# A VMamba block with attention and an fp8 feed-forward on one core: convolution split between two engines, opposite scan directions added before the transposes

## The chip, the cores and the metric

The kernel runs on one core of a Trainium2 chip. The metric is the time of one execution on the device, in microseconds (us). The core has five engines that run side by side and wait for one another through semaphores: TensorE (PE in the profile, its weight loads PEld), VectorE (DVE), ScalarE (ACT), GpSimd (POOL) and SyncE (SP, which here issues every DMA).

## The reference, cut to what matters

The input is eight images of 96 channels and 64 x 64 points. A group norm comes first, then a layer over the image with four scan directions, then linear attention and a feed-forward net with numbers rounded to 8 bits.

```python
xh = _layernorm(transpose(x), norm_w, norm_b)
xz = xh @ in_proj_w.T + in_proj_b            # 96 -> 2 x 192
xi, z = split(xz, 2)
xi = silu(conv3x3_depthwise(xi, conv_w) + conv_b)
xs = [x_hw, x_wh, flip(x_hw), flip(x_wh)]    # four directions, 4096 steps each
dts, Bs, Cs = split(einsum('bkdl,kcd->bkcl', xs, x_proj_w), ...)
delta = softplus(einsum(dts, dt_proj_w) + dt_proj_b)
# per step: h = exp(delta*A) * h + (delta*u) * B ;  y = sum_n h * C   (16 states)
y = out_y[0] + flip(out_y[2]) + T(out_y[1]) + T(flip(out_y[3]))   # back in image order
y = _layernorm(y) * silu(z)
x = x + y @ out_proj_w.T + out_proj_b
# then: t += attention(norm(t)); t += ffn(norm(t))
```

What the reader needs of it: the convolution is depthwise, that is, each channel is a sum of nine shifted copies of itself, each times one number. And the four directions' results are only ever added together; directions 0 and 2 run over the same order of points (forwards and backwards), and so do 1 and 3.

## The kernel before, in words

The kernel takes the images two at a time, in four passes (`for pair in range(npair)`). A pass has five stages, one after the other: `front`, `prepare`, `scan`, `back` and `tail`. Data goes between most of them through scratch in device memory (`zs`, `us`, `dl`, `du`, `bs`, `cs`, `ys`).

Outside the scan, a planner at build time decides the order of each engine's instructions. It starts from the order in which the code emits them and moves an instruction ahead when it judges its inputs and buffers to be ready. Inside `scan`, `tc.manual_schedule()` makes each engine take the scan's own instructions in the order written.

`front` holds the two images' 192 channels in three tiles of 128 rows: T=0 has channels 0 to 127 of image 0, T=1 the same of image 1, and T=2 the last 64 channels of both. `half(T)` picks the weights, and is the same for T=0 and T=1. Each image goes through group norm and layer norm in chunks of 512 points (L261 to L270: mean away on TensorE, square, variance on TensorE, Ln at L267, Exp at L268, product). Ln with a factor and Exp make the reciprocal root. Then each image's projection is written with a border of zeros into `pad[T]` (L283, L288), and `z` goes through Silu (L300) to `zs`. The convolution is done on TensorE: `diag` (L226) holds for each of nine taps a diagonal matrix of its weights; for each tile T and each of eight chunks nine matmuls add up in one bank (L311), and Silu takes it out into `xi[T]` (L316). An fp32 matmul is two instructions in the profile.

`prepare` stores `xi` to `us` (L323, L326), makes delta, delta times u, B and C for each direction (L356 to L391), and writes all of it to scratch. Delta takes Softplus on ScalarE (L372). After its loops a request for ScalarE's table set for ln and exp, `nc.scalar.preload_act_table_set(LOGEXP)`, is emitted (L397). The same request stands once at the kernel's start (L66). A function that the loaded set lacks gets a load in front of it, which the profile shows as ACT_TABLE_LOAD at that function's line.

`scan` goes over 128 steps (four directions, 32 pieces of 128 points). A step has eight slots `v`. In slot v TensorE and ScalarE make a decay `da` two slots ahead (L533, Exp at L537), in even slots GpSimd makes an input `dbu` for two slots (L515, with the start values copied on ScalarE at L512), and VectorE runs one scan (L548) into `h`. `h` has two buffers, one per step. Alongside, `sums(s - 1, f)` multiplies the previous step's `h` with C on TensorE (L566), eight parts f = 0 to 7, one a slot; after f = 3 and f = 7 ScalarE takes the bank `yp` out (L574). The buffer of `h` is free for step s+1 only when f = 7 of step s-1 is done. `store` writes `ys`.

`back` goes over 16 blocks (eight chunks, two images). It loads `zt`, `ut`, `xr` and then `yk`, which holds all four directions' y of the block, with points along the rows (L653, L659; two buffers). For each half g of the channels, 64 matmuls with the identity turn the pieces of `yk` round and add all four directions up in one bank `py` (L674), on top of D times u (L665). Then follow copies (L679, L681), the layer norm (L687 to L699, Ln and Exp at L698 and L699), the gate (L703, L706), the output projection (L709) and the residual (L712).

`tail` normalises again (`norm`, L729 to L737, Ln and Exp at L735 and L736), forms k and v and their product over all points, and then goes through the feed-forward in blocks of 512 points.

Of the kernel before, what the change touches and what calls it, by code (L numbers as in the profile page):

```python
# [51 lines left out]
def vss_attn_ffn(ctx: ExitStack, tc: tile.TileContext, a: dict):  # L52
# [164 lines left out]
    def front(pair, xi, zs, ybuf):  # L217
        with ExitStack() as st:
            p1 = st.enter_context(tc.tile_pool(name="p1", bufs=1))
            tmp = st.enter_context(tc.tile_pool(name="p1t", bufs=2))  # L220
            ps = st.enter_context(tc.tile_pool(name="p1ps", bufs=4, space=PSUM))

            diag = p1.tile([128, 2, 9, 128], F32, name="diag")
            for j in range(2):
                for t in range(9):
                    nc.vector.tensor_scalar(  # L226
                        diag[:, j, t, :], ident, convw[:, j, t : t + 1], None, ALU.mult
                    )
            pad = [t.rearrange("p (h w) -> p h w", w=HH + 2) for t in ybuf]
            for t in ybuf:  # L230
                nc.gpsimd.memset(t, 0.0)

            xts = []
            for b in range(2):
                xt = p1.tile([DIM, L], F32, name="xt", bufs=2)
                xts.append(xt)
                nc.sync.dma_start(xt, x[2 * pair + b])
                bst = tmp.tile([DIM, NCH, 6], F32, name="bst")
                for c in range(NCH):
                    nc.vector.bn_stats(bst[:, c, :], xt[:, bass.ts(c, F)])  # L240
                mv = tmp.tile([DIM, 2], F32, name="mv")
                nc.vector.bn_aggr(mv, bst.rearrange("p c s -> p (c s)"))
                gps = ps.tile([128, F], F32, name="gps", tag="ps")
                nc.tensor.matmul(gps[:DIM, 0:1], gmat, mv[:, 0:1], start=True, stop=True)
                gm = tmp.tile([DIM, 1], F32, name="gm")
                nc.vector.tensor_copy(gm, gps[:DIM, 0:1])
                gd = tmp.tile([DIM, 1], F32, name="gd")
                nc.vector.tensor_tensor(gd, mv[:, 0:1], gm, ALU.subtract)
                gv = tmp.tile([DIM, 1], F32, name="gv")
                nc.vector.scalar_tensor_tensor(gv, gd, gd, mv[:, 1:2], ALU.mult, ALU.add)  # L250
                vps = ps.tile([128, F], F32, name="vps", tag="ps")
                nc.tensor.matmul(vps[:DIM, 0:1], gmat, gv, start=True, stop=True)
                gr = tmp.tile([DIM, 1], F32, name="gr")
                nc.scalar.activation(gr, vps[:DIM, 0:1], AF.Ln, bias=eps5[:DIM])
                nc.scalar.activation(gr, gr, AF.Exp, scale=-0.5)
                nc.vector.tensor_scalar(xt, xt, gm, gr, ALU.subtract, ALU.mult)

                for c in range(NCH):
                    cs = bass.ts(c, F)
                    cps = ps.tile([128, F], F32, name="cps", tag="ps")  # L260
                    nc.tensor.matmul(cps[:DIM], c96, xt[:, cs], start=True, stop=True)  # L261
                    sq = tmp.tile([DIM, F], F32, name="sq")
                    nc.scalar.activation(sq, cps[:DIM], AF.Square)
                    vp = ps.tile([128, F], F32, name="vp", tag="ps")
                    nc.tensor.matmul(vp[:DIM], j96, sq, start=True, stop=True)
                    rs = tmp.tile([DIM, F], F32, name="rs")
                    nc.scalar.activation(rs, vp[:DIM], AF.Ln, bias=eps5[:DIM])  # L267
                    nc.scalar.activation(rs, rs, AF.Exp, scale=-0.5)  # L268
                    nc.vector.tensor_tensor(xt[:, cs], cps[:DIM], rs, ALU.mult)
                    nc.vector.tensor_scalar(xt[:, cs], xt[:, cs], nw, nb, ALU.mult, ALU.add)  # L270


            for b in range(2):
                xt = xts[b]
                lo = slice(64 * b, 64 * b + 64)
                for c in range(NCH):
                    cs = bass.ts(c, F)
                    r0 = c * ROWS
                    pm = ps.tile([128, F], F32, name="pm", tag="ps")
                    nc.tensor.matmul(pm, winT[:, 0:128], xt[:, cs], start=True, stop=True)  # L280
                    pl = ps.tile([128, F], F32, name="pl", tag="ps")
                    nc.tensor.matmul(pl[lo], winT[:, 128:DI], xt[:, cs], start=True, stop=True)
                    nc.scalar.activation(  # L283
                        pad[b][:, r0 + 1 : r0 + 1 + ROWS, 1 : HH + 1],
                        pm.rearrange("p (h w) -> p h w", w=HH),
                        AF.Identity, bias=inb[:, 0:1],
                    )
                    nc.scalar.activation(  # L288
                        pad[2][lo, r0 + 1 : r0 + 1 + ROWS, 1 : HH + 1],
                        pl[lo].rearrange("p (h w) -> p h w", w=HH),  # L290
                        AF.Identity, bias=inb[lo, 1:2],
                    )
                    zt = tmp.tile([DIM, 2, F], F32, name="zt")
                    for g in range(2):
                        pz = ps.tile([128, F], F32, name="pz", tag="ps")
                        nc.tensor.matmul(
                            pz[:DIM], winT[:, DI + g * DIM : DI + (g + 1) * DIM], xt[:, cs],
                            start=True, stop=True,
                        )
                        nc.scalar.activation(  # L300
                            zt[:, g], pz[:DIM], AF.Silu, bias=inz[:, g]
                        )
                    nc.sync.dma_start(zs[b, :, :, cs].rearrange("g p l -> p g l"), zt)

            for T in range(3):
                for c in range(NCH):
                    r0 = c * ROWS
                    pc = ps.tile([128, F], F32, name="pc", tag="ps")
                    for t in range(9):
                        dy, dx = divmod(t, 3)  # L310
                        nc.tensor.matmul(  # L311
                            pc, diag[:, half(T), t, :],
                            pad[T][:, r0 + dy : r0 + dy + ROWS, dx : dx + HH],
                            start=(t == 0), stop=(t == 8),
                        )
                    nc.scalar.activation(  # L316
                        xi[T][:, bass.ts(c, F)], pc, AF.Silu, bias=convb[:, half(T) : half(T) + 1]
                    )

    def spread(dst, T, src):  # L320

# [7 lines left out]
    def prepare(xi, us, dl, du, bs, cs_):  # L329
        with ExitStack() as st:  # L330
# [8 lines left out]
            for o in range(2):  # L339
                for c in range(NCH):  # L340
# [12 lines left out]
                    for k in (o, o + 2):  # L353
# [12 lines left out]
                        for T in range(3):  # L366
# [27 lines left out]
                                .rearrange("j a p t -> p (j a) t"),  # L394
                                T, dp.rearrange("p j a t -> p (j a) t"),
                            )
            nc.scalar.preload_act_table_set(LOGEXP)  # L397


    def scan(dl, du, bs, cs_, ys):  # L400
        with ExitStack() as st:
            st.enter_context(tc.manual_schedule())
            one = st.enter_context(tc.tile_pool(name="s1", bufs=1))
            wk = st.enter_context(tc.tile_pool(name="s2", bufs=2))
            trio = st.enter_context(tc.tile_pool(name="s3", bufs=3))
# [196 lines left out]
            for s in range(N + 2):  # L602
                for v in range(8):
# [4 lines left out]
                            drive(p // 2 + 2)  # L608
                        run(p)
                    if 0 < s <= N:  # L610
                        sums(s - 1, v)
                    if s < N:
                        if v == 0:
                            load(s + 1)
# [13 lines left out]
    def back(pair, ys, us, zs, t1):  # L628
        with ExitStack() as st:
# [6 lines left out]
            for c in range(NCH):  # L636
                cs = bass.ts(c, F)
                for b in range(2):
# [11 lines left out]
                    for k in range(KD):  # L650
                        v = ys[k, 8 * b : 8 * b + 8]
                        if k % 2 == 0:
                            nc.sync.dma_start(  # L653
                                yk[:, k], v[:, cs].rearrange("s (p j) e -> p s (j e)", j=4)
                            )
                        else:
                            v = v.rearrange("s (w g j) e -> g w s (j e)", w=HH, j=4)
                            for g in range(2):
                                nc.sync.dma_start(  # L659
                                    yk[64 * g : 64 * g + 64, k], v[2 * c + g]  # L660
                                )
                    yt = tmp.tile([128, 2, F], F32, name="yt")
                    for g in range(2):
                        py = psy.tile([128, F], F32, name="py")
                        nc.tensor.matmul(py, dpad[:, g], ut[:, g], start=True, stop=False)  # L665
                        for k in range(KD):
                            for j in range(4):
                                for e in range(4):
                                    o = py[32 * e : 32 * e + NE]
# [2 lines left out]
                                    else:  # L672
                                        o = o.rearrange("p (g j w) -> p g j w", g=2, j=4)[:, :, j]
                                    nc.tensor.matmul(  # L674
                                        o, yk[:, k, 4 * g + e, NE * j : NE * j + NE], ident,
                                        start=False, stop=(k + j == KD + 2),
                                    )
                        if g == 0:
                            nc.vector.tensor_copy(yt[:, g], py)  # L679
# [277 lines left out]
```

## Time and profile before

| | us |
|---|---|
| median of 3 runs | 13196.79 |
| lowest, highest | 13184.92, 13217.89 |
| span of the profiled execution | 13189.4 |
| busy: TensorE, VectorE | 9569.7, 8359.3 |
| busy: GpSimd, ScalarE | 7825.5, 7498.9 |

The first pass, by the times at which its stages change over in the trace:

| stage | from | to | length |
|---|---|---|---|
| `front`, norms (with the kernel's constants) | 0 | 158 | 158 |
| `front`, projection | 158 | 237 | 79 |
| `front`, convolution | 237 | 424 | 187 |
| `prepare` | 424 | 755 | 331 |
| `scan`, start | 755 | 780 | 25 |
| `scan` | 780 | 2712 | 1932 |
| `back` | 2712 | 3010 | 298 |
| `tail` | 3010 | 3345 | 335 |

How to read it: the busy times are sums over stages with different limits, so none of them says what bounds the kernel. The scan is well over half of a pass. Within a stage, the question is which engine, transfer or chain of waits sets the pace there. In rows of the profile, `x128` is a count, the number after the bar is busy time in us, then the mean in ns, and after the second bar stands the idle time of the engine just before these instructions and what ended it.

### The profile page before, as it was taken

What the parts mean: (1) busy time and instruction counts of PE and PEld (TensorE: products, weight loads), DVE (VectorE), ACT (ScalarE), POOL (GpSimd) and SP (SyncE); (2) the same over time, 40 slices, a digit from 0 to 9 for tenths busy, and PEclk for the clock granted to TensorE, in tenths of its full rate; (3) what the DMA queues carried; (4) which work ended last, traced back from release to release, by engine and by line L of the source; (5) the groups of instructions that cost most, each with busy time, mean ns of one, the idle gap of its engine ahead of it and who ended that gap; (6) DMA issues with size and microseconds to landing.
All of it is one profiled execution on the core that took longest, in us unless ns stands there. A gap on an engine that the chain in (4) does not pass through costs nothing. (4 is left out here: it accounts for less than half of the span.)

```text
span 13189.4 us, 405730 instructions
## 1 busy us (share of the span) xinstructions
PE 9569.7 (73%) x179456; PEld 6167.3 (47%) x179456; DVE 8359.3 (63%) x6293; ACT 7498.9 (57%) x12586; POOL 7825.5 (59%) x2686
## 2 busy tenths in 40 slices
PE   7966666687796666668779566666868956666686
PEld 2245555553224555555322455555533245555553
DVE  2378988932137999992213799899221389999822
ACT  2456666635445666663544666666254566666625
POOL 0379999910037999990003799999000389999900
PEclk9778888896777888889677788888967688888896
DMA  2788888861178888886017888888601888888860
GB/s 60 158 198 197 198 196 199 197 139 23 38 160 200 198 199 204 200 200 138 9 37 178 199 202 196 197 202 196 128 11 41 177 201 200 197 200 202 188 127 10
DMA packets 1627316, 2043.74 MB, mean 155 GB/s; under 512 B 958083, under 2 KB 1303252, under 8 KB 1622740
## 3 DMA queue, kind: packets, MB, share of 16 engines
q1 hardware_dynamic: 1625556, 2017.78, 66.8%
q8 instruction: 1408, 23.07, 0.8%
q14 instruction: 352, 2.88, 0.1%
HBM read 1579.00 MB, written 438.38 MB: 153 GB/s over the span
## 5 line engine op out<-in xcount | busy, mean ns | idle before, releaser
L515 POOL TENSOR_TENSOR dbu<-dut,bc 128x1536 f32<-128x1536 f32 x2048 | 7083.1, 3506 | 602.9 <-ACT dbu L512 516.2
L548 DVE TENSOR_TENSOR_SCAN h<-da,dbu 128x774 f32<-128x774 f32 x4096 | 6973.8, 1756 | 732.9 <-ACT da L537 419.2
L537 ACT ACTIVATE da<-da 128x768 f32<-128x768 f32 x4096 | 3263.9, 797 | 2210.4 <-PE da L533 2161.8
L566 PE MATMUL yp<-h,cw 128*32 128x48 f32 x131072 | 3172.0, 242 | 925.7 <-issue 911.4
L533 PE MATMUL da<-dm,aw 128*128 128x128 bf16 x24576 | 2424.9, 244 | 1736.8 <-DVE h L548 1384.4
L566 PEld LDWEIGHTS yp<-h,cw 128*32 128x32 f32 x131072 | 2534.7, 153 | 1519.2 <-issue 1191.2
L533 PEld LDWEIGHTS <-aw 128*128 128x128 bf16 x24576 | 1825.1, 108 | 1994.5 <-issue 1649.4
L469 ACT ACTIVATE cw<-bc,blk 128x512 f32<-128x512 f32 x2048 | 1478.3, 723 | 268.0 <-DMA bc<-cs 240.4
L348 POOL COPY u<-xi 128x512 f32<-128x512 f32 x96 | 110.1, 1160 | 1517.7 <-PE pc L311 1486.8
L391 POOL TENSOR_TENSOR dp<-rest,dp 128x512 bf16<-128x512 f32 x384 | 458.4, 1194 | 713.6 <-ACT dp L390 701.2
L742 POOL MEMSET tn<- 1x4096 f32 x8 | 27.8, 3506 | 1311.4 <-DVE t L712 1311.4
L376 DVE TENSOR_TENSOR du<-delta,xi 128x512 f32<-128x512 f32 x192 | 133.0, 692 | 1060.9 <-ACT delta L372 772.5
L812 POOL TENSOR_TENSOR ot<-t,y 96x512 f32<-96x512 f32 x64 | 73.5, 1148 | 1176.2 <-DVE y L810 1150.2
L311 PE MATMUL pc<-y,diag 128*128 128x512 f32 x1728 | 742.3, 592 | 0.0
L389 DVE TENSOR_TENSOR rest<-delta,dp 128x512 f32<-128x512 f32 x384 | 303.9, 792 | 662.7 <-ACT dp L388 662.7
L368 PE MATMUL pq<-S,dtw 12*128 12x512 f32 x768 | 582.2, 866 | 122.7 <-ACT delta L372 75.3
L574 ACT ACTIVATE yev<-yp 128x384 f32<-128x384 f32 x1024 | 500.0, 488 | 198.5 <-PE yp L566 185.4
L674 PEld LDWEIGHTS py<-ident,yk 128*24 128x24 f32 x16384 | 449.3, 103 | 177.9 <-issue 176.6
L674 PE MATMUL py<-ident,yk 128*24 128x128 f32 x16384 | 509.8, 275 | 23.9 <-issue 23.5
L311 PEld LDWEIGHTS pc<-y,diag 128*128 128x128 f32 x1728 | 326.4, 189 | 415.4 <-issue 415.4
L316 ACT ACTIVATE xi<-pc,c_convb 128x512 f32<-128x512 f32 x96 | 66.0, 687 | 675.8 <-PE pc L311 675.8
L681 ACT ACTIVATE yt<-py 128x512 f32<-128x512 f32 x64 | 38.2, 597 | 721.0 <-PE py L674 670.7
(133 smaller groups left out, 7591.7 us busy)
## 6 DMA issues: line engine op xcount, KB each, us to landing
dut<-du SPq DMA_DIRECT2D x1024, 768.0 KB
dm<-dl SPq DMA_DIRECT2D x512, 576.0 KB
dl<-dp SPq DMA_DIRECT2D x256, 384.0 KB
dm<-dl SPq DMA_DIRECT2D x512, 192.0 KB
ys<-yev SPq DMA_DIRECT2D x1024, 96.0 KB
du<-du SPq DMA_DIRECT2D x256, 256.0 KB
bc<-bs SPq DMA_DIRECT2D x512, 128.0 KB
bc<-cs SPq DMA_DIRECT2D x512, 128.0 KB
```

What stands on the lines that cost most here:

```text
L311: nc.tensor.matmul(pc, diag[:, half(T), t, :], pad[T][:, r0 + dy : r0 + dy + ROWS, dx : dx + HH], start=(t == 0), stop=(t == 8),)
L368: nc.tensor.matmul(pq, dtw[64:76, k, T], S[64:76], start=True, stop=True)
L389: nc.vector.tensor_tensor(rest, d, dp[:, :, 0], ALU.subtract)
L391: nc.gpsimd.tensor_tensor(dp[:, :, 2], rest, dp[:, :, 1], ALU.subtract)
L469: nc.scalar.activation(cw[i % 2][:, :, :, m, :].rearrange("p z j t -> p (z j) t"), bc[i][:, 1].rearrange("p z (j t) -> p (z j) t", j=NB), ...
L515: nc.gpsimd.tensor_tensor(segs(t)[:, :, :, 1:], dut[g // 2][:, NI * (r % 2) : NI * (r % 2) + NI, :].unsqueeze(1) .to_broadcast([128, 2, NI ...
L533: nc.tensor.matmul(e[:, i], aw[k, r][:, i, z, :], dm[s][:, NI * r + i, :], start=True, stop=True,)
L537: nc.scalar.activation(e, e, AF.Exp)
L548: nc.vector.tensor_tensor_scan(hs[s][:, w, r][:, d], da[p % 3][:, o : o + W6][:, d], dbu[4 * s + r][:, w][:, d], 0.0, ALU.mult, ALU.add,)
L566: nc.tensor.matmul(y[32 * q : 32 * q + 32, 2 * NE * i : 2 * NE * i + 2 * NE] .rearrange("p (j r i) -> p i j r", j=2, r=NR), w[:, z, :, t], ...
L574: nc.scalar.activation(yev[s][:, :, o : o + 8, :].rearrange("p j i e -> p i j e"), y[:, 0 : 16 * NE].rearrange("p (i j e) -> p i j e", j=2 ...
L674: nc.tensor.matmul(o, yk[:, k, 4 * g + e, NE * j : NE * j + NE], ident, start=False, stop=(k + j == KD + 2),)
```

## The change

Four parts.

1. The request for the table set moves from the end of `prepare` to the first line of `scan`, inside the order written out by hand. It is for having Exp in the scan and the later Ln and Exp in one set.
2. The convolution is split. T=1 stays on TensorE. T=0 and T=2 are done on VectorE, tap by tap over the whole tile: nine operations, each a shifted view of `pad[T]` times one weight per row, from the second on added to what is there. Silu then runs in place on ScalarE. T=0 is emitted between the two images' projections, T=2 after them, T=1 last. `diag` holds nine matrices instead of eighteen.
3. In the scan the sums run up to one slot earlier: slot 0 has f = 0 and 1, slots 1 to 6 have f = 2 to 7, slot 7 none.
4. In `back`, direction 2 is added to direction 0 on VectorE and direction 3 to direction 1 on GpSimd, in `yk`, before the transposes, which then go over two directions instead of four.

```diff
-            diag = p1.tile([128, 2, 9, 128], F32, name="diag")
-            for j in range(2):
-                for t in range(9):
-                    nc.vector.tensor_scalar(
-                        diag[:, j, t, :], ident, convw[:, j, t : t + 1], None, ALU.mult
-                    )
+            diag = p1.tile([128, 9, 128], F32, name="diag")
+            for t in range(9):
+                nc.vector.tensor_scalar(
+                    diag[:, t, :], ident, convw[:, 0, t : t + 1], None, ALU.mult
+                )
...
+            def taps(T):
+
+                for t in range(9):
+                    dy, dx = divmod(t, 3)
+                    w = convw[:, half(T), t : t + 1]
+                    v = pad[T][:, dy : dy + HH, dx : dx + HH]
+                    o = xi[T].rearrange("p (h w) -> p h w", w=HH)
+                    if t == 0:
+                        nc.vector.tensor_scalar(o, v, w, None, ALU.mult)
+                    else:
+                        nc.vector.scalar_tensor_tensor(o, v, w, o, ALU.mult, ALU.add)
+                for c in range(NCH):
+                    xc = xi[T][:, bass.ts(c, F)]
+                    nc.scalar.activation(
+                        xc, xc, AF.Silu, bias=convb[:, half(T) : half(T) + 1]
+                    )
...
-            for T in range(3):
-                for c in range(NCH):
...
+                if b == 0:
+                    taps(0)
+
+            taps(2)
+            for c in range(NCH):
...
+                    nc.tensor.matmul(
+                        pc, diag[:, t, :], pad[1][:, r0 + dy : r0 + dy + ROWS, dx : dx + HH],
+                        start=(t == 0), stop=(t == 8),
+                    )
+                nc.scalar.activation(xi[1][:, bass.ts(c, F)], pc, AF.Silu, bias=convb[:, 0:1])
...
-            nc.scalar.preload_act_table_set(LOGEXP)
...
     def scan(dl, du, bs, cs_, ys):
         with ExitStack() as st:
             st.enter_context(tc.manual_schedule())
+            nc.scalar.preload_act_table_set(LOGEXP)
...
                     if 0 < s <= N:
-                        sums(s - 1, v)
+                        for f in ((0, 1), (2,), (3,), (4,), (5,), (6,), (7,), ())[v]:
+                            sums(s - 1, f)
...
+                    nc.vector.tensor_tensor(yk[:, 0], yk[:, 0], yk[:, 2], ALU.add)
+                    nc.gpsimd.tensor_tensor(yk[:, 1], yk[:, 1], yk[:, 3], ALU.add)
...
-                        for k in range(KD):
+                        for k in range(2):
...
-                                        start=False, stop=(k + j == KD + 2),
+                                        start=False, stop=(k + j == 4),
```

More of the change, by code (lines that the diff above doesn't have):

```diff
@@ L303, in front @@
                     nc.sync.dma_start(zs[b, :, :, cs].rearrange("g p l -> p g l"), zt)
-            for T in range(3):
-                for c in range(NCH):
[L307 to L317, printed above, removed]
+                if b == 0:
+                    taps(0)
+            taps(2)
+            for c in range(NCH):
+                r0 = c * ROWS
+                pc = ps.tile([128, F], F32, name="pc", tag="ps")
+                for t in range(9):
+                    dy, dx = divmod(t, 3)
+                    nc.tensor.matmul(
+                        pc, diag[:, t, :], pad[1][:, r0 + dy : r0 + dy + ROWS, dx : dx + HH],
+                        start=(t == 0), stop=(t == 8),
                     )
+                nc.scalar.activation(xi[1][:, bass.ts(c, F)], pc, AF.Silu, bias=convb[:, 0:1])
     def spread(dst, T, src):
```

## The prediction

> **What bounds the kernel now.** No engine bounds the whole. The work comes in stages, four times over (one pass for each pair of images), so I first split the first pass by the view of busy time by stretch. The columns are length, then busy time of TensorE, weight load, VectorE, ScalarE and GpSimd, then granted clock, DMA share and GB/s.
>
> ```profile
> 237.00:424.00 187.00, 186.22 (x435) 81.73 (x434) 0.00 (x0) 17.70 (x26) 0.69 (x1) 1.00 0.06 25
> 424.00:755.00 331.00, 270.69 (x384) 71.19 (x384) 143.58 (x197) 188.79 (x321) 142.01 (x121) 0.67 0.96 210
> 2720.00:2980.00 260.00, 235.52 (x3854) 140.31 (x3853) 54.86 (x79) 74.75 (x93) 0.00 (x0) 0.99 0.72 141
> 80.68:158.28 77.60, 59.85 (x67) 16.00 (x68) 32.67 (x47) 30.07 (x50) 0.00 (x0) 1.00 0.06 24
> 3369.26:3464.46 95.20, 59.78 (x67) 16.00 (x68) 28.63 (x44) 73.08 (x85) 0.00 (x0) 0.50 0.00 0
> ```
>
> The reader is to see four things. The convolution (first line) is TensorE alone, 186 of 187 us, with VectorE idle. `prepare` (second) is bound by DMA, share 0.96, so moving it earlier doesn't change its length. `back` (third) is TensorE at 90% with DMA at 0.72. The last two lines are the same work, the two layer norms of `front`, in pass 0 and pass 1: 77.6 against 95.2 us, and the difference is ScalarE, 30 against 73 us busy.
>
> The groups by line explain that difference and price the other parts.
>
> ```profile
> L735 ACT ACT_TABLE_LOAD x128 | 164.2, 1283 | 2.3
> L267 ACT ACT_TABLE_LOAD x48 | 61.6, 1283 | 0.9
> L66 ACT ACT_TABLE_LOAD x1 | 1.3, 1283 | 0.7 <-PEq L946 0.7
> L256 DVE TENSOR_SCALAR xt<-xt,gm,gr 96x4096 f32<-96x4096 f32 x8 | 19.2, 2406 | 18.3 <-ACT gr L255 18.3
> L706 DVE SCALAR_TENSOR_TENSOR g<-g,c_onb,z 96x512 f32<-96x512 f32 x128 | 89.7, 740 | 0.0
> ```
>
> Every one of the 128 runs of L735 has a load in front of it (and so its twin L736); L267 loads in 48 of 64 chunks, that is in passes 1 to 3. In pass 0 the set asked for at L66 served both Ln and Exp.
>
> In the scan VectorE is the bound, and the waits name what it loses:
>
> ```profile
> DVE h L548 <- ACT da L537: 419.2, 244, 17.8
> DVE h L548 <- PE yp L566: 238.6, 158, 4.8
> ```
>
> The four scans last 1921, 1899, 1899 and 1910 us, and VectorE is busy for 1743 us of the first. The second wait is for the sums that free an `h` buffer.
>
> **What the Trainium skill says.** "ScalarE: Activation LUTs", section "Table sets: the hidden batching unit", lists one set with both exp and ln; pass 0 agrees. Its section "What ACT_TABLE_LOAD costs" gives 1283 ns plus a drain of about 1380; here the load is 1283 ns and the Exp behind it starts at once, so I charge 1.28 us. "VectorE: DVE Perf Modes", section on the perf-mode tier table, gives fp32 tensor_scalar twice the rate of two-input operations; L256 (4096 elements in 2.41 us) agrees. "GPSIMD Engine Reference", section "Performance versus the Vector engine", calls two-input adds about twice as slow; here 512 elements cost 1.15 us at L812 against 0.69 on VectorE.
>
> **The change, part by part.**
>
> *Convolution.* Before, each pass runs 432 matmul instructions back to back; one chunk of 18 ends every 7.72 us, 24 chunks are 185.4 us. Afterwards T=1 stays on TensorE: 8 x 7.72 = 61.8 us. T=0 and T=2 become nine VectorE passes each over 4096 elements. The first is a tensor_scalar, 2.41 us. The other eight read two tensors; the trace has this form only at 512 elements, 0.74 us. Its lower bound is 2.41 us, its upper 8 x 0.74 = 5.9 us. A two-input add of 512 takes 0.69 us, which is the page's (N+151)/0.96 ns; for 4096 that estimate is 4.42, and with the 0.05 that this form costs more, 4.47 us. A tile is 2.41 + 8 x 4.47 = 38.2 us (bounds 22 and 50). In pass 0 image 0's plane is complete at 205.5 us (its eighth L283), so T=0 runs from 205.5 to 244 beside image 1's projection, T=2 from 244 to 282, and its eight Silu (0.69 each) end at 287.5. TensorE starts T=1 at 237 and ends at 299, Silu included 299.5. `prepare` waits for the later, TensorE: 299.5 instead of 423.8, a gain of 124. Even at 50 us a tile VectorE ends at 306 + 5.5. The stores of `xi` sit in one queue: T=2's 2 MB used to fall into the DMA-bound stage, now T=1's does, and T=2's too if it queues behind T=1, up to 10 us. I take 121, four times: -484.
>
> *diag.* Nine builds fewer. In pass 1, 18 take 14.3 us because most wait for the GpSimd memsets (11.1 us). What goes is nine at the free rate of 0.2: -2 in three passes, -6; in pass 0 it is hidden behind the first load.
>
> *Sums one slot earlier.* f=7 used to run in slot 7, just before the next step's first scan overwrites that `h`. Now it runs in slot 6, one scan (1.75 us) earlier. Listing the idle time in the four scans, waits on yp sum to 241 us, and only 48 of it exceeds 1.75 us a piece. So 193 us can go. Slot 0 gets twice the sums (2 x 0.69 + 0.42 = 1.8 us, about one scan) and ScalarE has copy and eviction in the same slot; neither is queued before the exp that VectorE needs next. The same stalls of TensorE (gaps of 2 to 4 us marked "issue") also hold up `da`, which takes part of it back. I take -165, bounds -60 and -200.
>
> *y added first.* Per block `back` now has a steady period of 18.09 us. 128 of its 256 transposing matmuls go at 28.5 ns each (206 in 5.88 us): 3.65 us. Of the period 1.25 us is TensorE waiting for `g`, so TensorE needs 18.09 - 3.65 = 14.4 us. The adds are 768 elements: VectorE (768+151)/0.96 = 0.96 us, GpSimd 1.5 x 1.15 = 1.73 us; both engines have room. The add is a new wait: the next block's copies and `g` queue behind it on VectorE. DMA is busy 0.72 x 18.09 = 13.0 us a block, at `prepare`'s best share 13.6. And there is a loop over two blocks, as `yk` has two buffers and its load queues behind `xr`, which waits for L712: from L712 about 10.5 us until 2.2 MB at 200 GB/s have landed, then GpSimd's add 1.75, the transposes left 3.7, copy 0.65, yc 3.7, square to variance 1.5, Ln, load and Exp 2.6, g 2.8, po and t 2.0: 29.2 us, 14.6 a block. I take 15.0: -3.1 x 64 = -198. Nothing gained and the full 13.6 are the ends: 0 and -287.
>
> *Table request.* The old request at L397 has no row in any pass: it reads and writes nothing, so nothing held it behind `prepare`'s Softplus. In the scan's written-out order it precedes the scan's ScalarE work, but nothing precedes it there. The timeline shows that this order doesn't hold work behind `prepare`: the scan's first VectorE memset runs between `prepare`'s operations.
>
> ```profile
> 736.14 0.69 DVE L376 TENSOR_TENSOR du<-delta,u 128x512 f32<-128x512 f32 x1 [0.18 <-DMA du<-du]
> 737.49 0.91 DVE L413 MEMSET da<- 128x1024 f32 x1 [0.65 <-ACT delta L372]
> 740.46 0.67 DVE L389 TENSOR_TENSOR rest<-delta,dp 128x512 f32<-128x512 f32 x1
> ```
>
> So the likelier case is that the request floats away again: 0.
>
> Sum: 13197 - 484 - 6 - 165 - 198 = 12344 us.
>
> **Rivals.** *The request stays in place.* For it: it does now precede the scan's first Exp. Then `front` of passes 1 to 3 falls to pass 0's time, 3 x 17.6 = 53. The scan's start saves 4 x 1.3 = 5. In `tail`'s second half Ln's load ends before its input is there and only Exp's lies on the chain: 16 x 1.28 = 20.5 a pass. In its first half the second image's square queues behind the first's loads, two loads a chunk: 8 x 2.7 = 21.6. That is 168 in all. `back` drops 0.6 a block, 38. Together 264: 12080 us.
>
> *`back` gains nothing*, because VectorE's add waits for `yk` with the running block's copy behind it, the period staying at 18.1: 12344 + 198 = 12542 us. For it: the load lands about 10.5 us after L712 while the copy comes 4.2 us after it. Against it: the planner has put the other VectorE work behind its inputs well.
>
> *Slower.* Every load, add and chain of `back` in series is 12.9 + 18.7 = 31.6 us a block, 13.5 more, 864 in all; with nothing gained in the scan and only half in the convolution (242, and 6 for diag): 13197 + 864 - 248 = 13813 us. Against it: two `yk` buffers, and VectorE is busy only 55 of 260 us here.
>
> **How the numbers follow.** Forecast 0.53, request in place 0.33, no gain in `back` 0.11, slower 0.03. The forecast's own bounds (165 +35/-105, 198 +90, conv +-40) put it at 12220 to 12480; the request's case reaches 11960 with `back` near 13.6 us a block. The range 11960 to 12560 holds the first three nearly whole and leaves out the slow case and the far ends. All but the slow case are over 6% from before, so faster 0.96, same 0.01, slower 0.03.
>
> **What would show it.** Right: two VectorE rows of taps near 4.5 us, 576 matmuls left of 1728, `prepare` starting about 300 us into pass 0; waits of the scan on yp under 80 us; 8192 transposes and a period near 15 us; table loads as before. Wrong: loads gone from L698, L735 and their twins (then 12080); a tap over 5.9 us; ScalarE's Silu of T=0 ahead of image 1's evictions, with TensorE idle in the projection; new waits of VectorE on `yk`.

## The result

The kernel after takes 12637.14 us (median of 4 runs, 12632.21 to 12676.64), the kernel before 13197.52 (median of 4). The ratio is 0.958, 95% interval 0.956 to 0.960: 560 us less. The forecast was 12344, so 293 us of its gain are missing; 12637 is also 77 us above its range.

The profile after, in the same views as before. First the busy time by stretch (length, then TensorE, weight load, VectorE, ScalarE, GpSimd, granted clock, DMA share, GB/s): projection, the rest of the convolution, `prepare`, a piece of `back`.

```profile
158.00:237.00 79.00, 79.00 (x163) 25.68 (x162) 40.74 (x12) 47.08 (x68) 0.00 (x0) 1.00 0.27 80
237.00:289.00 52.00, 51.22 (x121) 21.96 (x119) 36.42 (x9) 14.79 (x24) 3.64 (x4) 1.00 0.24 81
289.00:612.00 323.00, 267.43 (x378) 69.25 (x376) 143.04 (x197) 188.66 (x321) 137.71 (x117) 0.68 0.96 212
2580.00:2840.00 260.00, 213.09 (x2081) 106.11 (x2080) 72.29 (x98) 81.08 (x101) 25.22 (x14) 0.87 0.69 140
```

The convolution, 187 us of TensorE alone before, has become 52 us after the projection, with VectorE busy beside it in both lines. `prepare` has kept its DMA share of 0.96 and its length (326 us from its first to its last instruction, 325 before). In `back` TensorE has fallen from 235 to 213 busy us of 260, and the granted clock with it, from 0.99 to 0.87.

The groups by line, for the new operations and the table loads:

```profile
L282 DVE SCALAR_TENSOR_TENSOR xi<-y,c_convw,xi 128x4096 f32<-128x4096 f32 x64 | 285.2, 4482 | 1.4
...
L755 ACT ACT_TABLE_LOAD x128 | 164.2, 1283 | 2.3
...
L681 POOL TENSOR_TENSOR yk<-yk 128x768 f32<-128x768 f32 x64 | 115.3, 1802 | 1087.0 <-DMA yk<-ys 868.9 <-PE py L685 113.3 <-DMA ut<-us 29.9
...
L267 ACT ACT_TABLE_LOAD x48 | 61.6, 1283 | 0.9
...
L680 DVE TENSOR_TENSOR yk<-yk 128x768 f32<-128x768 f32 x64 | 60.6, 946 | 91.7 <-DMA yk<-ys 91.7
```

A tap takes 4.48 us and waits for nothing. The adds cost 0.95 and 1.80 us. Every table load of before is still there (L755 is `norm`'s Ln, L267 the Exp of `front`).

VectorE's waits in the scan, to be held against 419.2 us for `da` and 238.6 for `yp` before:

```profile
DVE h L564 <- ACT da L553: 519.6, 271, 18.2
...
DVE h L564 <- PE yp L582: 37.9, 24, 4.0
...
DVE h L564 <- ACT dbu L528: 33.7, 30, 3.7
```

The wait for the sums is gone, as forecast; the wait for the decays has grown by 100 us, and one for the start values of `dbu` has come, which was 0.2 us before.

Where the 560 us come from is seen in the stages. The table has them for all kernels of this study, worked out from the first and last instruction of each stage in the trace and summed over the four passes (norms are `front` up to the projection; about 130 us between `prepare` and the scan are left out).

| kernel | norms | projection to end of `prepare` | scan | `back` | `tail` |
|---|---|---|---|---|---|
| before | 515 | 2333 | 7636 | 1296 | 1278 |
| after | 510 | 1819 | 7610 | 1284 | 1274 |
| e1 sums alone | 515 | 2345 | 7615 | 1301 | 1270 |
| e2 adds alone | 515 | 2326 | 7628 | 1284 | 1273 |
| e3 convolution alone | 510 | 1823 | 7649 | 1307 | 1276 |
| e4 request pinned | 456 | 1838 | 7611 | 1164 | 1052 |
| e5 ahead, two buffers | 509 | 1837 | 7624 | 1142 | 1266 |
| e6 ahead, three buffers | 510 | 1840 | 7647 | 951 | 1267 |
| e7 three buffers alone | 510 | 1835 | 7629 | 1316 | 1279 |
| e8 even sums | 510 | 1855 | 7595 | 1279 | 1274 |
| e9 half the sums | 510 | 1838 | 7435 | 1269 | 1274 |
| e10 no sums | 509 | 1855 | 7445 | 1252 | 1276 |
| e11 ahead, no add | 510 | 1835 | 7634 | 1187 | 1274 |
| e12 together | 457 | 1851 | 7630 | 936 | 1052 |

The convolution gave 514 us where 484 were forecast. The scan gave 26 for 165, `back` 12 for 198. So there are two questions: what became of the waits taken out of the scan, and why halving the transposes did nothing for `back`.

The timeline of `back` shows the second one at work. This is one block of the kernel after (start, length, then engine, line, operation; idle time before it in brackets):

```profile
2647.26 0.33 SPq L664 DMA_DIRECT2D xr<-in_x_dram  x1
2647.70 0.38 SPq L670 DMA_DIRECT2D yk<-ys  x1
...
2658.76 0.63 ACT L719 ACTIVATE yrs<-yrs 96x512 f32<-96x512 f32 x1
2659.22 1.80 POOL L681 TENSOR_TENSOR yk<-yk 128x768 f32<-128x768 f32 x1 [17.45 <-DMA yk<-ys]
2659.42 1.40 DVE L723 SCALAR_TENSOR_TENSOR g<-yc,c_onw,yrs 96x512 f32<-96x512 f32 x2 [8.33 <-ACT yrs L719]
2660.75 1.48 DVE L726 SCALAR_TENSOR_TENSOR g<-g,c_onb,z 96x512 f32<-96x512 f32 x2
...
2661.62 3.01 PE L729 MATMUL po<-g,c_woT 96*96 96x512 f32 x4 [3.30 <-DVE g L726]
2662.16 0.94 DVE L680 TENSOR_TENSOR yk<-yk 128x768 f32<-128x768 f32 x1
...
2664.56 4.28 PE L694 MATMUL py<-ident,yk 128*24 128x128 f32 x128
2664.67 0.75 DVE L732 SCALAR_TENSOR_TENSOR t<-po,c_outb,xr 96x512 f32<-96x512 f32 x1 [1.57 <-PE po L729]
```

Read it from the end. All 128 rows of transposes of the next block stand behind `po` of this one, and VectorE's add for them stands behind `g`. Before, some 50 of 256 rows lay ahead of `po`:

```profile
2852.73 1.07 PE L674 MATMUL py<-ident,yk 128*24 128x128 f32 x32
2853.73 1.12 PE L665 MATMUL py<-ut,dpad 96*128 96x512 f32 x2
2854.79 0.83 PE L674 MATMUL py<-ident,yk 128*24 128x128 f32 x18
2856.87 1.96 PE L709 MATMUL po<-g,c_woT 96*96 96x512 f32 x4 [1.25 <-DVE g L706]
```

So the transposes that were saved had in part filled TensorE's wait for `g`, which has gone from 1.25 to 3.30 us. And `po` behind it takes 3.01 us in place of 1.96: the clock record of the trace stands at 0.5 from 2662.4 to 2665.8 us. Over all 64 blocks `po` has a granted clock of 0.60 in the mean and takes 3.26 us in the median; before it was 0.97 and 1.96 us. The wait and the slower `po` together use up 3.35 of the 3.65 us that the transposes were to save. Another thing is in the first two lines of the block: the `yk` loads are issued right after that of `xr`, which waited for `t` of an earlier block, and land 11.5 us later. Two suspects, then: the order on the engines, and the ring of loads.

### The profile page after: what moved, and what is told of

Same layout as the page of the kernel before. It is cut to its first block, busy times and chain, and to the rows that moved or that the text cites. A ratio compares the mean times of both kernels' runs of the same rounds, so it can differ in the third digit from the quotient of the medians.

```text
span 12630.4 us, 387420 instructions
## 1 busy us (share of the span) xinstructions
PE 8953.1 (71%) x170112; PEld 5798.8 (46%) x170112; DVE 8774.4 (69%) x6393; ACT 7447.1 (59%) x12586; POOL 7941.4 (63%) x2750
## 5 line engine op out<-in xcount | busy, mean ns | idle before, releaser
L582 PE MATMUL yp<-h,cw 128*32 128x48 f32 x131072 | 3131.2, 245 | 1075.3 <-issue 1060.3
L549 PE MATMUL da<-dm,aw 128*128 128x128 bf16 x24576 | 2498.9, 250 | 1519.1 <-DVE h L564 1131.1
L582 PEld LDWEIGHTS yp<-h,cw 128*32 128x32 f32 x131072 | 2539.1, 154 | 1632.0 <-issue 1364.9
L549 PEld LDWEIGHTS <-aw 128*128 128x128 bf16 x24576 | 1846.4, 111 | 1832.2 <-issue 1487.9
L681 POOL TENSOR_TENSOR yk<-yk 128x768 f32<-128x768 f32 x64 | 115.3, 1802 | 1087.0 <-DMA yk<-ys 868.9
L723 DVE SCALAR_TENSOR_TENSOR g<-yc,c_onw,yrs 96x512 f32<-96x512 f32 x128 | 89.9, 742 | 533.2 <-ACT yrs L719 533.2
L406 ACT ACTIVATE dp<-rest 128x512 bf16<-128x512 f32 x384 | 241.4, 630 | 326.0 <-DVE rest L405 326.0
L384 PEld LDWEIGHTS pq<-S,dtw 12*128 12x128 f32 x768 | 156.2, 244 | 552.1 <-ACT delta L388 188.1
L528 ACT COPY dbu<-h 128x12 f32<-128x12 f32 x1984 | 409.1, 206 | 0.0
L729 PE MATMUL po<-g,c_woT 96*96 96x512 f32 x256 | 205.7, 950 | 206.1 <-DVE g L726 206.1
L757 DVE TENSOR_TENSOR tn<-ncp,nrs 96x512 f32<-96x512 f32 x64 | 44.0, 687 | 424.5 <-ACT nrs L756 424.5
```

The lines of the kernel that those rows point to most:

```text
L384: nc.tensor.matmul(pq, dtw[64:76, k, T], S[64:76], start=True, stop=True)
L406: nc.scalar.activation(dp[:, :, 1], rest, AF.Copy)
L528: nc.scalar.copy(start, segs(hs[s - 1][:, :, r])[:, :, :, 1 if back else TC])
L549: nc.tensor.matmul(e[:, i], aw[k, r][:, i, z, :], dm[s][:, NI * r + i, :], start=True, stop=True,)
L582: nc.tensor.matmul(y[32 * q : 32 * q + 32, 2 * NE * i : 2 * NE * i + 2 * NE] .rearrange("p (j r i) -> p i j r", j=2, r=NR), w[:, z, :, t], ...
```

## The experiments

### Each part alone: e1, e2, e3

e1 is the kernel before with the sums' order of the change, and nothing else:

```diff
-                        sums(s - 1, v)
+                        for f in ((0, 1), (2,), (3,), (4,), (5,), (6,), (7,), ())[v]:
+                            sums(s - 1, f)
```

> The kernel before with the order of the y sums alone changed. The stages of the two profiles put the four scans 26 us apart, where the forecast had 165. Theory A (the sums' waits are gone, but TensorE's own halts are as many as before and now reach the scan through the decays): the time falls by 10 to 40 us, to about 13171; the scan waits for yp fall from 241 to about 38 us, those for da rise from 349 to about 450 us. Rival B (the order does save 165 us, and something else in the change, such as the clock or the transfers, takes it back): about 13032 us, and da stays near 350 us.

Measured: ratio 1.000, interval 0.9988 to 1.0012; four scans 7615 us. The order alone is worth nothing that the timing can tell. The scan's row (busy time, and after the second bar the idle time and what ended it) is nearly that of the kernel after. The rows are those of before, after and e1:

```profile
L548 DVE TENSOR_TENSOR_SCAN h<-da,dbu 128x774 f32<-128x774 f32 x4096 | 6973.8, 1756 | 732.9 <-ACT da L537 419.2
L564 DVE TENSOR_TENSOR_SCAN h<-da,dbu 128x774 f32<-128x774 f32 x4096 | 7025.8, 1760 | 656.5 <-ACT da L553 519.6
L548 DVE TENSOR_TENSOR_SCAN h<-da,dbu 128x774 f32<-128x774 f32 x4096 | 7027.8, 1760 | 658.8 <-ACT da L537 527.0 <-PE yp L566 36.6 <-ACT dbu L512 30.9
```

Rival B, some other part of the change taking the gain back, is out. Besides the waits that come back, the busy time rises by 54 us. In the trace 2618 of the 4096 scans before begin while the one ahead is still ending, and in e1 2335: this overlap shrinks from 218 to 180 us, and a scan lasts 4 ns longer. So part of what was taken from the waits came back as delays too short to be listed as waits.

e2 is the kernel before with the two adds and two directions in the transposes:

```diff
+                    nc.vector.tensor_tensor(yk[:, 0], yk[:, 0], yk[:, 2], ALU.add)
+                    nc.gpsimd.tensor_tensor(yk[:, 1], yk[:, 1], yk[:, 3], ALU.add)
...
-                        for k in range(KD):
+                        for k in range(2):
```

> The kernel before with the y of opposite directions added ahead of the transposes, and nothing else. Theory A (half the transposes are gone, but VectorE's add is queued behind g, so that no transpose is issued until po is done, where before 25 of 128 and the start of the next block lay there): the back's period stays near 18 us, the time falls by 0 to 25 us, to about 13187. Rival B (the transposes saved are worth what was forecast, and another part hides it): 198 us less, 12999, period about 15 us.

Measured: ratio 1.000, interval 0.998 to 1.002; `back` 1284 us, median period 18.2. As theory A has it.

e3 is the kernel after with sums, request and `back` as before, so that only the convolution and `diag` are changed.

> The kernel before with the convolution of two of the three channel tiles on VectorE, and nine diagonals in place of eighteen. Theory A (all that the change gained is here): 514 us less in the stretch from projection to the end of prepare, about 12684 us. Rival B (part of the gain seen there comes from the other edits): less than 480 us, over 12717.

Measured: ratio 0.963, interval 0.962 to 0.965; from projection to end of `prepare` 1823 us, 510 less. The whole time fell by 466 us, the spans of the two profiles by 494; in these its scans and `back` came out 13 and 11 us longer than before's, which is within what these stages vary by from kernel to kernel. So most of the gain is here, but not all: the change has 0.958 (0.956 to 0.960), which leaves 0.5% of the time, some 70 us, to its other parts, where e1 and e2 by themselves show nothing. In the table e3 and the kernel after differ by 39 us in the scan and 23 in `back`. Whether the other parts do a little more beside the new convolution was not tried.

### The table request: e4

```diff
-            nc.scalar.preload_act_table_set(LOGEXP)
+            tc.keep_in_program_order(nc.scalar.preload_act_table_set(LOGEXP))
```

This ties the request to follow the ScalarE instruction emitted before it, in issue order only.

> The kernel after with the table request of each scan pinned behind the ScalarE instruction traced before it. Theory A (the request as it stands is moved to the front of the program, so that every Ln and Exp of back, tail and the later fronts loads a table): of the table loads, those of norm's Ln and Exp (128 each), the back's (64 each) and the later fronts' (48 each) vanish; front 53, scan 5 and tail 168 us less as worked out in the prediction, and 64 blocks of the back by 2 x 1.28 us or more, since its period is now one chain: 164 us; together about 390 us, 12247 us. Rival B (as forecast, the back gains 38): 264 us less, 12373. Rival C (the loads were hidden): 12637 as after.

Measured: ratio 0.930, interval 0.928 to 0.932; 12254 us. All loads but these are gone from the groups by line:

```profile
L316 ACT ACT_TABLE_LOAD x4 | 5.1, 1283 | 0.1
L388 ACT ACT_TABLE_LOAD x4 | 5.1, 1283 | 0.1
L418 ACT ACT_TABLE_LOAD x4 | 5.1, 1283 | 0.1
```

Beside them there is one at the kernel's start, as before. L418 is the request itself, once a pass. The Trainium skill's page "ScalarE: Activation LUTs", section "Table sets: the hidden batching unit", has one set hold exp and ln; this run agrees, since no Ln or Exp after L418 loads a table until the next Silu. By stages, norms 53, `back` 120 and `tail` 222 us less. So the request of the change does float away, and where it stays it gives 383 us. Theory A had the sum within 7 us, though with 164 for `back` and 168 for `tail`.

### Order and ring in `back`: e5, e6, e7, e11

e5 takes the kernel after and emits `begin` (loads, adds, transposes) of the next block between Exp and `g` of this one, with two ties of issue order for each block:

```diff
+                nxt = begin(*work[n + 1]) if n + 1 < len(work) else None
...
+                    if nxt:
+                        behind(first, nxt[5])
...
+                    if nxt:
+                        behind(mm, nxt[6])
```

The first puts `g` behind the next block's add, the second `po` behind its last transpose.

> The kernel after; in the back each block's add on VectorE is put ahead of g of the block before, and its transposes ahead of that block's po; buffers as they are. Two theories of why the back kept its period of 18.05 us. Theory A (a ring through the loads: the yk loads are issued behind that of xr, which waits for t of two blocks earlier, and land 11.5 us later): with the transposes ahead of po the ring closes in one block, 0.45 + 11.5 + 1.8 (add) + 4.3 (transposes) + 2.5 (po) + 0.75 (t) = 21.3 us a block, 64 x 3.2 = 205 us slower than after, 12840. Theory B (only the order on VectorE and TensorE is at fault): the transposes lie beside Ln, Exp and g, period 14 us, 64 x 4 = 259 us faster, 12378.

Measured: ratio 0.947, interval 0.944 to 0.950; `back` 1142 us, median period 15.9. Neither theory's number: order alone gives 142 us, but the ring is there too. Which of the two ties does it was not tried. The timeline of e5:

```profile
2703.58 0.75 DVE L755 SCALAR_TENSOR_TENSOR t<-po,c_outb,xr 96x512 f32<-96x512 f32 x1 [3.15 <-DMA yk<-ys]
...
2704.35 0.33 SPq L663 DMA_DIRECT2D xr<-in_x_dram  x1
...
2704.73 0.58 SPq L675 DMA_DIRECT2D yk<-ys  x1
...
2712.29 1.81 POOL L680 TENSOR_TENSOR yk<-yk 128x768 f32<-128x768 f32 x1 [14.60 <-DMA yk<-ys]
...
2714.16 1.95 PE L694 MATMUL py<-ident,yk 128*24 128x128 f32 x64 [1.09 <-POOL yk L680]
...
2716.03 1.96 PE L750 MATMUL po<-g,c_woT 96*96 96x512 f32 x4
...
2718.03 0.75 DVE L755 SCALAR_TENSOR_TENSOR t<-po,c_outb,xr 96x512 f32<-96x512 f32 x1 [2.04 <-PE po L750]
```

From `t` to `t` it runs through the load of `xr`, the `yk` loads behind it, GpSimd's add, half the transposes and `po`: 14.45 us here, closed in one block as theory A said. It is shorter than 21.3 because the planner put the first two pieces of `yk` ahead of `xr`, so the rest lands 7.6 us after its issue, and only 64 rows of transposes wait for it.

e6 is e5 with the ring opened:

```diff
-                zt = tmp.tile([DIM, 2, F], F32, name="z3")
+                zt = tmp.tile([DIM, 2, F], F32, name="z3", bufs=3)
...
-                xr = tmp.tile([DIM, F], F32, name="xr")
+                xr = tmp.tile([DIM, F], F32, name="xr", bufs=3)
```

> As e5_ahead_two, with three buffers in place of two for z and xr, so that the yk loads are not issued behind a wait for t of the block two before. Theory A (order and ring both bind, each alone keeps the period): period 13.5 us (from yc to the end of po: 2651.15 to 2664.6 in the profile of after) to 15, since loads of 2.36 MB a block at the 198 GB/s of the scan take 12: some 230 us faster than after, 12400. Theory B (order alone): the same time as e5_ahead_two. Rival C (the transfers bind at their 18 us rate whatever the order): 12637.

Measured: ratio 0.935, interval 0.931 to 0.938; `back` 951 us, median period 12.45, below the 13.5 to 15 expected. Theory A's mechanism holds, order and ring both bind, though its "each alone keeps the period" does not: order alone had given 142 us. The transposes now run beside Ln, Exp and `g`, and both TensorE and the DMA engines are full (the view of busy time by stretch):

```profile
2640.00:2780.00 140.00, 138.43 (x1631) 73.43 (x1630) 55.57 (x78) 62.78 (x78) 19.85 (x11) 1.00 1.04 191
```

e7 is the kernel after with the three buffers alone:

> The kernel after with three buffers for z and xr alone, order as it is. If the serial order (transposes of a block behind po of the one before) is a limit by itself: the back keeps its 18 us a block, 1284 us in all, and the time is after's 12637. If the ring of loads alone sets it: period 14 to 16.4 us, the back 1030 to 1180 us.

Measured: 12701 us in one run, `back` 1316. Nothing gained: with the transposes behind `po` the block is one chain whatever the loads do. The chain of the kernel after is the period: from one block's transposes at 2646.38 to the next's at 2664.56 is 18.2 us.

e11 is e6 with all four directions transposed and no add:

> The kernel e6_ahead_three with the y of opposite directions not added: 256 transposes a block in place of 128, ahead of po, three buffers for z and xr. If the adds are worth what the forecast gave them once order and ring no longer bind: TensorE needs 4.3 us more than the 12.45 of e6_ahead_three, 16.7 a block, the back 951 + 64 x 4.3 = 1226 us, the time 275 us longer. If the adds are worth nothing there either (transfers bind): the back stays at 951.

Measured: 12576 us in one run, `back` 1187, median period 16.3. TensorE is the bound there:

```profile
2640.00:2820.00 180.00, 178.47 (x3033) 109.25 (x3026) 45.83 (x66) 60.59 (x76) 0.00 (x0) 1.00 0.75 156
```

So the adds are worth 236 us to `back`, 3.8 us a block, once order and ring let TensorE be the bound. The forecast's price for the transposes, 3.65 us, was right for that kernel, not for the one that it was put into.

### The scan's waits: e8, e9, e10

Theory A is that TensorE halts at times, and that the sums' order only chooses where the halt shows. Before, 550 waits of TensorE marked "issue" in the scan cost it 1056 us (L566 and L533); after, 633 cost 1224 (L582 and L549):

```profile
PE yp L566 <- issue: 911.4, 470, 6.0
PE da L533 <- issue: 145.0, 80, 4.4
...
PE yp L582 <- issue: 1060.3, 544, 6.0
PE da L549 <- issue: 163.5, 89, 4.7
```

In the trace after, TensorE stands still for over 1.5 us 387 times in the four scans, and in 376 of these a transfer of the queue that carries instructions runs. Of stretches of 2.5 us taken at random in these scans, 61% meet such a transfer, so this is more than chance.

e8 spreads the sums more evenly, 3, 2, 2, 2, 2, 3, 2 and 0 sixteenths of a step in slots 0 to 7:

```diff
-                        for f in ((0, 1), (2,), (3,), (4,), (5,), (6,), (7,), ())[v]:
-                            sums(s - 1, f)
+                        sums(s - 1, range((0, 3, 5, 7, 9, 11, 14, 16)[v], (3, 5, 7, 9, 11, 14, 16, 16)[v]))
```

> The kernel after with the sixteen parts of a step's y sums spread 3, 2, 2, 2, 2, 3, 2, 0 over the eight slots in place of 4, 2, 2, 2, 2, 2, 2, 0. Theory A (TensorE's halts of 2.5 us at the fetch of instructions are as many, and each reaches the scan by one way or another): the four scans stay within 20 us of after's 7610. Theory B (the double portion in slot 0 delays the decays of slots 2 to 5, where the waits rose by 0.35 us a step): the scans lose 100 us or more, 7500 or less, the time is 12530.

Measured: ratio 0.959, interval 0.956 to 0.962; scans 7595 us, 15 less than after. The double portion in slot 0 was not it.

e9 and e10 take matmuls away, so that TensorE has fewer instructions to fetch. The output of e9 lacks half of the terms of y, that of e10 all of them:

```diff
-                    for z in range(2):
+                    for z in range(1):
```

```diff
-                for i in range(2 * (f % 4), 2 * (f % 4) + 2):
+                for i in range(0):
```

> The kernel after with the y sums of one state of each pair left out: 128 of 256 sum matmuls of a step go, the rest, the evictions and the scans stay; the output lacks half of its terms. A step has 176 matmuls in place of 304. Theory A (the scan's waits over 0.5 us, 506 us in four scans, follow TensorE's halts at the fetch of its instructions, 387 over 1.5 us): halts and waits fall with the number of matmuls, to about 225 halts and 290 us; the four scans take 7610 - 215, 7395 us. Theory B (the waits come from the decays' own ring of three buffers and would be there without halts): over 450 us of waits, scans over 7560.

> The kernel after with the matmuls of the y sums left out altogether (48 matmuls a step stay; the evictions copy zeros). Theory A: under 70 halts, under 100 us of waits over 0.5 us, scans 7200 us. Theory B: over 450 us of waits, scans over 7560.

Measured, in one run each: 12461 and 12472 us, scans 7435 and 7445. The halts go further than I expected, from 633 waits marked "issue" to one of 0.5 us, but the scan doesn't follow. ScalarE's wait in the kernel after:

```profile
ACT cw L485 <- DMA bc<-cs: 260.9, 151, 26.4
```

and in e9, where only half of the sums are left:

```profile
ACT cw L485 <- DMA bc<-cs: 914.3, 251, 26.7
...
PE yp L582 <- issue: 0.5, 1, 0.5
```

ScalarE now waits for the `bc` loads in 251 places, at the copies that build `cw`, and Exp stands behind these in its queue. I took every wait of VectorE over 0.5 us in front of a scan and asked what had come last before it (us over four scans, worked out from the trace; a halt is a wait of TensorE over 0.5 us marked "issue" in the 4 us before, and the sums of rounded figures can be 1 off):

| what came last | before | after | e8 | e9 | e10 |
|---|---|---|---|---|---|
| not Exp but the sums | 273 | 28 | 31 | 0 | 0 |
| Exp, after a decay late by a halt of TensorE | 252 | 359 | 374 | 0 | 0 |
| Exp, after a decay late without a halt (mostly for its weights, `aw`) | 12 | 19 | 21 | 54 | 49 |
| Exp, behind an eviction that waited for sums | 30 | 55 | 3 | 0 | 0 |
| Exp, behind `cw` copies that waited for `bc` | 15 | 44 | 30 | 371 | 431 |
| sum | 583 | 506 | 458 | 425 | 480 |

Theory A is right on the halts, and neither theory on what the scans gain. Halts do set most of the waits of before and after (rows 1, 2 and 4). The change took 245 us from the waits for the sums, and 107 of them came back at the decays, 25 behind evictions and 29 behind `cw` copies. But with the halts gone a second cause, the `bc` loads, takes over: in e9 these waits are only 81 us less than after. The scans get 175 us shorter, the rest of it from shorter delays (3106 scans begin before the one ahead has ended, 2366 after). Whether the loads are late for their buffers or for the rate of the transfers (DMA share 0.88 there) was not tried.

### All together: e12

The kernel after with e4's tie, e6's order and buffers and e8's sums.

> The kernel after with the request pinned, each block's add and transposes ahead of the block before, three buffers for z and xr, and the even order of the y sums. If the gains add up but for the back, where the transfers hold 12.4 us a block: e4's 12247 less (1164 - 940) less 15, about 12010 us, 0.911 of before. If pinning and order gain the same thing twice: no shorter than e4's 12254 less 100.

Measured: 12031 us, ratio 0.912, interval 0.910 to 0.915, 606 us below the kernel after. `back` keeps e6's median period of 12.45 us although its table loads are gone, with DMA at 1.05 of its engines, so there pinning and order do overlap. The norms and `tail` keep what e4 gave; e8's 15 us in the scan are not seen again.

## Why the prediction was wrong

*Convolution and diag: right.* A tap took 4.48 us where 4.47 was estimated, and TensorE ended last, at 284.5 us in pass 0 where 299 was forecast. That it was earlier is luck: the last `pm` of the projection came at 220 us and not at 235, since the projection's matmuls, half as fast at first (four of `pz` in 3.73 us, later in 1.96), went to full speed at some 167 us in this run and at 197 in that of before, where the first records of the clock stand; T=1 itself took 61.9 us for 61.8. The stretch gained 514 us over the passes, not 484; but in the kernels of the table with this convolution it takes 1819 to 1855 us and in those without it 2326 to 2345, so the 30 us beyond the forecast are no more than it varies by. The norms, with the diagonals in them, lost 5 where 6 were forecast.

*Table request: right.* That "the likelier case is that the request floats away again: 0" has come true, the loads are where they were. The rival that it stays was the larger prize: e4 gives 383 us where the rival had 264. Norms were 53 as worked out; `tail` was 222 for 168, which the runs do not split further. `back` was 120 for 38, 1.9 us a block. Of this 1.28 us are the load ahead of Exp, which lies on the chain that is now the period; the load ahead of Ln is over when `yv` ends and cost 0.1. The rest goes with `po`, 2.38 us in the median where it took 3.26 in the kernel after.

*Sums: the size was wrong.* The waits on `yp` fell by 201 us, 193 were forecast. The term that failed is "which takes part of it back": I allowed 28 us for it, and it took nearly all. The waits for decays grew by 100 us, those for the start values of `dbu` by 34, and VectorE's busy time in the scans by 52, because fewer scans begin before the one ahead has ended. The two profiles differ by 26 us; over all kernels with the change's order the scans take 7610 to 7647, without it 7628 to 7649, and e1's timing has 1.000. I had seen that TensorE's halts hold up the decays too, and still counted a wait as lost time that its removal gives back. A decay runs two scans ahead at most, so a halt that the scan no longer meets at the sums it can meet at the next decay.

*y added first: the step was wrong.* "TensorE needs 18.09 - 3.65 = 14.4 us" takes TensorE as the bound of `back`, with a fixed wait of 1.25 us for `g`. That it was busy for 90% of the stretch didn't make it so: part of that work was filling time behind a chain. The planner put VectorE's add behind `g` and all transposes behind `po`, and the saved 3.65 us became 2.05 us more of waiting for `g` and 1.3 us more of `po` at a lower clock. (The "steady period of 18.09 us" was also that of the shorter blocks; the median before is 18.58, after 18.05.) The rival "`back` gains nothing" has the right size for this part, but another reason: VectorE waits for `yk` only 91.7 us in 64 blocks, and no copy is held up. The ring of loads that I had worked out at 29.2 us for two blocks was not the bound after; it becomes one in e5.

The missing 293 us are these two (139 and 186), less the 30 us that the convolution showed beyond its forecast. No case of the prediction had both small at once: its own lower ends for the two, -60 and 0, would have made 12647 us.

## What to carry to other kernels

Work taken off a busy engine saves time only if it isn't filling a wait: look at what stands ahead of and behind the instruction that waits, in the order of the changed kernel, and look to the order and the buffers along with the cut. Here the cut alone gave 12 us in `back`, order and buffers without it 109 (e11 against before), and both together 345 (e6). When a wait is caused by a stall of another engine, ask where that stall shows next before counting the wait as won. An instruction without operands, like the request here, has to be tied to a place, or what it is for doesn't happen.

## What the runs showed of the hardware

- TensorE's halts in the scan, 1.9 us in the mean (1224 us in 633), come with transfers of the instruction queue, and vanish in e9, where a step has 176 matmuls in place of 304.
- TensorE's clock was lower where it had less to do. From 1000 to 2000 us the kernel after has it at 0.83 with 20330 matmuls in 683 busy us; e9 has it at 0.51 with 12105 in 694, e10 at 0.50 with 3276 in 438. So e9 has 40% fewer instructions than after and no less busy time: a decay's matmul takes 306 ns in the mean there, in the kernel after 250. In e9 the clock is at 0.5 from 586 us, before the scan begins, and from 1000 to 2000 us it comes up three times, for 3.4 us each.
- The Trainium skill's page "TensorE: Matmul & The Clock Gate", section "HAM oscillation — how this bites in real kernels", asks for no gap over 3.4 us. That alone does not tell these two kernels apart: e9 has 6 such gaps from 1000 to 2000 us, the kernel after 17. What would have brought e9's clock back is not shown.
- A longer wait can cost more than its own length. In `back` the wait for `g` grew from 1.25 to 3.30 us, and the four matmuls of `po` behind it went from 1.96 to 3.26 us in the median, at a mean granted clock of 0.60 for 0.97. In e6, where `po` waits for nothing, they take 1.96 us again.
